# Two layers on one Trainium2 core: a group's query transfers issued earlier at the start of the attention stage, and output products and values moved in front of transposes in its last two slots

## The chip, the cores and the metric

The program runs on one core of a Trainium2 chip, in one launch, all in float32. The metric is the device time of one execution in microseconds (us). The kernel before took 937.56 us (median of three runs, 935.68 to 938.08).

The engines are named as the profile names them: PE is TensorE (PEld its weight loads), DVE is VectorE, ACT is ScalarE, POOL is GpSimd, SP is SyncE, which here only issues transfers (DMAs). Each engine works through its own list of instructions in order and waits on semaphores for the others.

## The reference, cut to what matters

The input x has 16 sequences of 256 tokens with 256 features. Two layers each compute `x = x + s * silu(f)` from the layer-normed x. In the first, s is a linear recurrence with a complex diagonal state of 32 and f is an MLP with GELU. In the second, s is attention with 16 heads whose keys and values come from a latent of 64 per token, and f is a linear layer with a routed low-rank addition. The change touches the attention only:

```
q = (x @ Wq).reshape(B, S, N_HEADS, QK_DIM)
q = concatenate([q_nope, apply_rope(q_rope)], -1)
scores = einsum('bqhd,bkhd->bhqk', q, k) * scale        # k: latent part and 64 roped features
scores = where(tril(ones((S, S))), scores, min)          # causal
attn = softmax(scores, -1)
out = einsum('bhqk,bkhd->bqhd', attn, v).reshape(B, S, N_HEADS * V_DIM)
s = out @ Wo
x = x + s * silu(f)
```

The kernel folds the key and value matrices into the query and output weights, so that queries and values live in the latent of 64.

## The kernel before, in words

The 4096 tokens are cut into 8 chunks of 512 (two sequences each). Layer 1 runs first, over all chunks. From about 276 us on the attention stage runs: for each chunk four groups of four heads, and for each group two units, one for each sequence. That is 8 units for a chunk and 64 in all, and one slot of the loop at line 1488 for each unit.

A group's queries are made on PE in four products (`query_mm`, tile pq). Two give the latent part, which ACT scales into the tile qg (`query_lat`). Two give the roped part: DVE multiplies them (`query_mul`, tile qmul), POOL adds the products into qrot (`query_rot`), and `query_move` copies qrot into the other rows of qg by eight DMAs on SP's queue. A group's queries are made in the odd slot before and the even slot of the group ahead, so group 2, which slot 4 uses first, gets its products in slots 1 and 2 and its moves in slot 2. There are two qg buffers and one for qrot.

A unit's scores come in three packs of query blocks (`score_pack`, tile sc in PSUM, three buffers): blocks 7 and 6, then 5 to 3, then 2 to 0. For each pack PE multiplies, DVE adds the mask and takes the maxima, ACT takes the exponentials into pr with their sums. DVE's reciprocal of the sums and POOL's multiplications (`normalise`) finish the probabilities.

The probabilities have to be turned before the values can be multiplied. For units 0 to 61 DVE turns 32x32 blocks (`turn`, tile turned, two buffers), SP writes them to DRAM by four DMAs (`send`, tile far), and one slot later SP reads them back by one DMA (`fetch`, tile pT, four buffers). For the last two units PE transposes them instead (`turn_here`, tile pt), and ACT and DVE copy the result to pT. `values` multiplies pT with the latent rows of the keys (tile av) and a copy writes attT. In even slots from 4 on, the values of the units four and three slots back are taken. `finish_mm` multiplies attT with the output weights (tile po, eight products of 128x256 for each 128 tokens), and `finish_out` multiplies by the gate and adds x. In the slots with r = 3, 4, 5 and 7 of a chunk this is done for one 128-token tile each of the chunk before; the last chunk's follow after the loop.

The order of the work is written by hand. The wrapper `InOrder` keeps the instructions of each engine, and SP's transfers, in the order in which the Python code calls them. All instructions of the stage therefore carry one line, L53, in the profile, and groups are told apart by their tiles. SP's order in an even slot is: the fetch of the unit two back, the four sends of the unit one back, the eight moves of the next group. In an odd slot it is a fetch and four sends.

The tiles pq, tp, pkv, pk, pm, pt, av and po share five PSUM buffers (`m1`), sc has three others, and three of the last chunk's four po tiles take sc buffers.

Of the kernel before, what the change touches and what calls it, by code (L numbers as in the profile page):

```python
# [28 lines left out]
NPAIR = NH // 2  # L29
# [12 lines left out]
def tile_two_layers(ctx: ExitStack, tc: tile.TileContext, d: dict, out: bass.AP):  # L42
# [158 lines left out]
    def bc(ap, n):  # L201

        return ap.unsqueeze(1).to_broadcast([ap.shape[0], n, ap.shape[1]])

    def bc_in(ap, n):

        return ap.unsqueeze(2).to_broadcast([ap.shape[0], ap.shape[1], n])
# [16 lines left out]
    def m1(name, shape):  # L224
        return place["pool"].tile(shape, F32, tag=place["tag"], name=name)
# [67 lines left out]
    def kv_end(ch):  # L293
        k = chunks[ch]
        sq = k.tmp[:, 0]
        ve.tensor_tensor(sq, k.pkv[:, :, 0:KVL], bc_in(k.rk, KVL), ALU.mult)
        ve.tensor_tensor(k.row[:, :, 0:KVL], sq, bc(kvw_bc, TPC), ALU.mult)
# [97 lines left out]
    def query_mul(n, t):  # L395
        q = groups[n]
        q.mul[t] = m = qm.tile([P, 2, CH], F32, tag="qmul", name=f"qmul_{n}_{t}")
        for r in range(2):
            ve.tensor_tensor(
                m[:, r, :].rearrange("p (b s) -> p b s", b=2),  # L400
                q.ps[t].rearrange("p (b s) -> p b s", b=2),
                bc(rot_q[:, r, :], 2), ALU.mult,
            )
# [15 lines left out]
    def query_move(n):  # L419
        q = groups[n]  # L420
        for r in range(2):
            for h in range(G):
                sp.dma_start(
                    q.qg[64 + 32 * r : 96 + 32 * r, :, h, :],
                    q.rot[32 * h : 32 * h + 32, r, :].rearrange("p (a q) -> p a q", q=32),
                )


    with ExitStack() as l0:
# [177 lines left out]
        for k in range(8):  # L607
            n = 1 << k
# [613 lines left out]
        ch = NCH - 1  # L1222
# [70 lines left out]
    def mid_chunk(ch):  # L1293
        k = chunks[ch]
        pmT = m1(f"pmT_{ch}", [P, CH])
        for j in range(TPC):
            pe.transpose(pmT[:, j * P : (j + 1) * P], k.mg[:, j, :], ident)
        k.mT = a2.tile([P, CH], F32, tag="mT", name=f"mT_{ch}", bufs=1)
        ac.copy(k.mT, pmT)
# [19 lines left out]
    def gate_end(ch, jp):  # L1319
        k = chunks[ch]  # L1320
        g = k.g2[:, 2 * jp : 2 * jp + 2, :]
        ve.scalar_tensor_tensor(g, g, 1.0, k.h, ALU.add, ALU.mult)
# [63 lines left out]
    def normalise(u, packs):  # L1386
        blocks = [a for pi in packs for a, _ in PACK[pi]]
        lo, hi = min(blocks), max(blocks) + 1
        ve.reciprocal(u.sr[:, lo:hi], u.sr[:, lo:hi])
        for a in blocks:  # L1390
            v = u.pr[:, OFF[a] : OFF[a] + 32 * (a + 1)]
            gp.tensor_scalar(v, v, u.sr[:, a : a + 1], 1.0, ALU.mult, ALU.mult)
# [27 lines left out]
    def new_pT(u):  # L1420
        u.pT = pp.tile([P, G, 3, P], F32, tag="pT", name=f"pT_{u.n}", bufs=4)

    def fetch(u):
        new_pT(u)
        sp.dma_start(u.pT, u.far.rearrange("k s h z q -> (k s) h z q"))

    def turn_here(u, z):

        if z == 1:
            new_pT(u)  # L1430
        a0, k0 = THIRDS[z]
        pt = m1(f"pt_{u.n}_{z}", [P, CH])
        for y in range(4):
            o = OFF[a0] + y * WID[a0] + 32 * k0
            pe.transpose(pt[:, y * P : (y + 1) * P], u.pr[:, o : o + P], ident)
        for y, e in ((0, ac.copy), (2, ve.tensor_copy)):
            e(
                u.pT[:, :, z, 32 * y : 32 * y + 64].rearrange("p h (a q) -> p a h q", q=32),
                pt[:, y * P : (y + 2) * P].rearrange("p (a h q) -> p a h q", a=2, h=G),
            )  # L1440

    def values(u, e=None):
        k, b = chunks[u.ch], u.b
        av = m1(f"av_{u.n}", [P, 2, S])
        for p2 in range(2):
            for kb in range(2):
                for hh in range(2):
                    h = 2 * p2 + hh
                    pe.matmul(
                        av[64 * hh : 64 * hh + 64, p2, P * kb : S].rearrange(  # L1450
                            "p (z s) -> p z s", s=P
                        ),
                        k.row[:, 2 * b + kb, 0:KVL],
                        u.pT[:, h, 2:3, :] if kb else u.pT[:, h, 0:2, :],
                        start=(kb == 0), stop=(kb == 1),
                    )
        if b == 0:
            k.attT.append(a2.tile([P, 2, CH], F32, tag="attT", name=f"attT_{u.n}", bufs=6))
        (e or ac.copy)(k.attT[u.g][:, :, b * S : (b + 1) * S], av)

    def finish_mm(ch, j, p0, p1):
        k = chunks[ch]
        if p0 == 0:
            if ch == NCH - 1 and j < 3:
                k.po[j] = ps_sc.tile([P, CH], F32, tag="sc", name=f"po_{ch}_{j}")
            else:
                k.po[j] = m1(f"po_{ch}_{j}", [P, CH])
        for p in range(p0, p1):
            pe.matmul(
                k.po[j][:, 0:D], k.attT[p // 2][:, p % 2, j * P : (j + 1) * P], wout[:, p, :],  # L1470
                start=(p == 0), stop=(p == NPAIR - 1),
            )

    def finish_out(ch, j, last=False):
        k = chunks[ch]
        tag, bufs = (("o", 2), ("o", 2), ("h", 1), ("tmp", 1))[j if last else 0]
        o = a2.tile([P, D], F32, tag=tag, name=f"o_{ch}_{j}", bufs=bufs)
        ve.tensor_tensor(o, k.po[j][:, 0:D], k.g2[:, j, :], ALU.mult)
        (ve if last else gp).tensor_tensor(o, o, X[ch][:, j, :], ALU.add)
        t0 = ch * CH + j * P  # L1480
        (sp if last else gp).dma_start(out_dram[t0 : t0 + P, :], o)
# [3 lines left out]
    LAST = NCH * PER  # L1485
    FINISH = (3, 4, 5, 7)
    units = [Unit(i) for i in range(LAST)]
    for i in range(LAST):
        ch, r = divmod(i, PER)
        odd = i % 2 == 1  # L1490
        u, w = units[i], units[i - 1] if i else None
        here = w is not None and w.i >= LAST - 2
        n = (i + 3) // 2 if odd else (i + 2) // 2
        n = n if n < len(groups) else None
        more = ch + 1 < NCH
        last = ch - 1 if ch and r in FINISH else None

        if 2 <= i:
            fetch(units[i - 2])
        score_pack(u, 0)  # L1500
        if w:
            normalise(w, (2,))
        if r == 1:
            gate_end(ch, 0)
        if r == 2:
            gate_end(ch, 1)
            if more and ch:
                norm_end(ch + 1)
        if r == 5 and more:
            kv_end(ch + 1)  # L1510
        if w:
            for z in (1, 2):
                turn_here(w, z) if here else turn(w, z)

        if r == 0:
            mid_chunk(ch)
        if r == 7 and more:
            key_chunk(ch + 1)
        if n is not None:
            query_mm(n, 0 if odd else 3)  # L1520
            if not odd:
                query_lat(n, 3)
        score_pack(u, 1)

        if odd and n is not None:
            query_mm(n, 1)
            query_mul(n, 0)
        if w:
            if here:
                turn_here(w, 0)  # L1530
            else:
                turn(w, 0)
                send(w)
        if not odd:
            if n is not None:
                query_move(n)
            if i >= 4:
                values(units[i - 4])
                values(units[i - 3])
        score_pack(u, 2)  # L1540
        normalise(u, (0, 1))

        if odd and n is not None:
            query_mm(n, 2)
            query_mul(n, 1)
            query_rot(n)
            query_lat(n, 2)
        if r < 2:
            gate_begin(ch, r)
        if r == 0 and more and ch:  # L1550
            norm_begin(ch + 1)
        if r == 2 and more:
            transpose_chunk(ch + 1)
        if r == 4 and more:
            kv_begin(ch + 1)
        if r == 6 and more:
            router_chunk(ch + 1)
        if last is not None:
            j = FINISH.index(r)
            finish_mm(last, j, 0, NPAIR)  # L1560
            finish_out(last, j)


    ch = NCH - 1
    u0, u1 = units[LAST - 2], units[LAST - 1]
    normalise(u1, (2,))
    turn_here(u1, 1)
    turn_here(u1, 2)
    values(units[LAST - 4])
    values(units[LAST - 3], ve.tensor_copy)  # L1570
    values(u0)
    turn_here(u1, 0)
    for j in range(TPC):
        finish_mm(ch, j, 0, 6)
    values(u1, ve.tensor_copy)
    for j in range(TPC):
        finish_mm(ch, j, 6, NPAIR)
# [76 lines left out]
```

## Time and profile before

| | |
|---|---|
| median of three runs | 937.56 us (935.68 to 938.08) |
| the profiled execution | 936.25 us, span 934.5 us |
| PE busy | 916.7 us, 98% of the span |
| DVE, POOL, ACT busy | 662.2, 471.9, 450.8 us |
| packets' time on SP's transfer queue (q1) | 52.7% of 16 engines' span |
| slot 0 to slot 8 of the attention stage | 276 to 346 us |
| slot 63 and the end | 898 to 934.5 us |

The span runs from the first to the last instruction of the profiled execution, and its time is the span and 1.75 us around it. In the timeline each row has start, length, engine, line, operation, tiles (written tile first), shape, number of records and, in brackets, the idle time of the engine before it and what ended it. A float32 matmul leaves two records on PE. A wait's releaser is inferred from the order of semaphore events; where the engine named had long been done, it was another, often a DMA. A transfer's time to landing is counted from the start of its issue.

### The profile page before, as it was taken

The page shows a single profiled execution, that of the slowest core. Times are in us where ns is not written, and L with a number is a line of the kernel's source. Part 1 is how long each engine was busy: PE and PEld are TensorE (multiplying, and loading weights), DVE is VectorE, ACT ScalarE, POOL GpSimd, SP SyncE. Part 2 cuts the span into 40 slices and gives each one's busy share as a digit, 9 for nine tenths or more (in the row PEclk, how much of TensorE's full clock was granted, in tenths as well). Part 3 has the DMA queues.
Part 4 walks back from the last instruction along what each step waited for, and adds up shares of the span by engine and source line. Part 5 has one row for each costly group of instructions (what it writes and reads, how often), then busy time and mean ns, then how long its engine had stood idle before and what let it go on. Part 6 is the DMA issues. An engine that isn't in the chain of part 4 may idle for free.

```text
span 934.5 us, 16539 instructions
## 1 busy us (share of the span) xinstructions
PE 916.7 (98%) x5066; PEld 688.2 (74%) x5066; DVE 662.2 (71%) x2005; ACT 450.8 (48%) x1495; POOL 471.9 (51%) x804
## 2 busy tenths in 40 slices
PE   8999999999999899999999999999999999999988
PEld 7765889887757567777777777777777777777766
DVE  6883668664688688678867866886886678686662
ACT  3333355554346455545645454564555456455450
POOL 1319166778255445545554554555455554645550
PEclk9999999999999999999999999999999999999999
DMA  9730000000024777776786777678677766866870
GB/s 279 224 114 1 1 1 1 1 1 1 1 32 117 182 217 199 204 178 167 174 228 164 189 195 194 165 173 230 165 197 181 197 168 169 231 166 174 224 201 29
DMA packets 196599, 133.93 MB, mean 143 GB/s; under 512 B 142304, under 2 KB 187168, under 8 KB 196512
## 3 DMA queue, kind: packets, MB, share of 16 engines
q1 hardware_dynamic: 194192, 128.68, 52.7%
q0 software_dynamic: 1344, 3.67, 1.0%
q8 instruction: 41, 0.67, 0.3%
q10 hardware_dynamic: 976, 0.53, 0.2%
q14 instruction: 46, 0.38, 0.1%
HBM read 63.11 MB, written 52.95 MB: 124 GB/s over the span
## 4 chain that ended last, share of the span: by engine, by line
PE 87%; DVE 5%; DMA 2%; SPq 2%; POOL 1%; issue 1%; ACT 1%; POOLq 0%; DVEq 0%; ACTq 0%
PE pq L53 21%; PE sc L53 14%; PE po L53 10%; PE av L53 9%; PE ph L53 6%; PE pf L53 6%; PE r L53 5%; PE pg L53 5%; PE f L53 4%; SPq L53 2%; PE pm L53 2%; PE tp L53 1%; PE pkv L53 1%; DMA far<-turned 1%; POOL pr L53 1%
## 5 line engine op out<-in xcount | busy, mean ns | idle before, releaser
L53 POOL TENSOR_SCALAR pr<-pr,sr 128x256 f32<-128x256 f32 (+7 forms) x512 | 192.5, 395 | 277.4 <-DVE sr L53 271.8
L53 ACT ACTIVATE pr<-sc,nm 128x256 f32<-128x256 f32 (+7 forms) x512 | 189.5, 380 | 279.9 <-DVE sr L53 197.0
L53 PEld LDWEIGHTS sc<-kT,qg 128*128 128x128 f32 x1024 | 159.3, 191 | 63.4 <-issue 40.0
L53 PE MATMUL sc<-kT,qg 128*128 128x256 f32 (+7 forms) x1024 | 175.7, 305 | 5.5 <-DMA qg<-qrot 2.9
L53 DVE STREAM_TRANSPOSE turned<-pr 128x512 f32<-128x512 f32 x186 | 123.3, 688 | 14.3 <-POOL pr L53 13.9
L53 DVE TENSOR_REDUCE nm<-sc 128x1 f32<-128x256 f32 (+7 forms) x512 | 127.7, 301 | 6.6
L53 PE MATMUL pq<-xnT,wlat 128*128 128x512 f32 x256 | 124.3, 609 | 0.0
L53 PE MATMUL pq<-xnT,wrope 128*128 128x512 f32 x256 | 120.2, 593 | 0.0
L53 PE MATMUL po<-wout,attT 128*128 128x256 f32 x512 | 115.8, 380 | 0.0
L53 PEld LDWEIGHTS po<-wout,attT 128*128 128x128 f32 x512 | 96.4, 190 | 20.9 <-issue 6.2
L53 ACT ACTIVATION_READ_ACCUMULATOR pr<-sc,nm 128x1 f32 x512 | 103.5, 202 | 0.0
L53 PE MATMUL av<-pT,row 128*64 128x256 f32 (+1 forms) x1024 | 90.5, 329 | 0.3 <-DMA pT<-far 0.3
L53 POOL TENSOR_TENSOR qrot<-qmul,qmul 128x512 f32<-128x512 f32 x64 | 83.4, 1324 | 5.1 <-DVE qmul L53 3.4
L53 DVE TENSOR_TENSOR sc<-sc,kmask 128x96 f32<-128x96 f32 (+1 forms) x192 | 45.9, 239 | 54.3 <-PE sc L53 52.9
L53 DVE TENSOR_TENSOR qmul<-pq,rot_q 128x512 f32<-128x512 f32 x128 | 80.9, 674 | 0.4 <-PE pq L53 0.4
L53 PEld LDWEIGHTS av<-pT,row 128*64 128x64 f32 x1024 | 64.2, 137 | 23.0 <-issue 0.5
L53 ACT ACTIVATE qg<-pq 64x512 f32<-64x512 f32 x128 | 75.4, 589 | 5.9 <-PE pq L53 5.2
L53 PEld LDWEIGHTS pq<-xnT,wlat 128*128 128x128 f32 x256 | 46.1, 192 | 32.2 <-issue 32.1
L53 PEld LDWEIGHTS pq<-xnT,wrope 128*128 128x128 f32 x256 | 45.7, 191 | 32.4 <-issue 32.1
L53 PE MATMUL ph<-xnT,p1T 128*128 128x512 f32 (+1 forms) x160 | 58.6, 524 | 0.8 <-DVE xnT L53 0.8
L53 PE MATMUL pf<-p2T,hT 128*128 128x256 f32 x256 | 56.8, 379 | 0.0
L53 PEld LDWEIGHTS pf<-p2T,hT 128*128 128x128 f32 x256 | 48.2, 190 | 7.2 <-issue 0.9
(216 smaller groups left out, 1227.2 us busy)
## 6 DMA issues: line engine op xcount, KB each, us to landing
far<-turned SPq DMA_DIRECT2D x248, 192.0 KB, 3.7
pT<-far SPq DMA_DIRECT2D x62, 768.0 KB, 4.7
qg<-qrot SPq DMA_DIRECT2D x256, 64.0 KB, 2.4
x<-in_x_dram SPq DMA_DIRECT2D x7, 512.0 KB, 9.3
out_dram<-o POOLq DMA_DIRECT2D x28, 128.0 KB, 3.3
wqn_wo<-in_wq_nopeT_dram SPq DMA_DIRECT2D x4, 512.0 KB, 4.7
wqn_wo<-in_Wo_dram SPq DMA_DIRECT2D x4, 512.0 KB, 5.8
p2T<-in_proj2T_dram SPq DMA_DIRECT2D x2, 512.0 KB, 8.0
```

Source lines behind the costliest of these rows:

```text
L53: r = getattr(self.engine, name)(*args, **kw)
```

## The change

It has three parts, all of them moves.

1. In slot 2 the eight moves of group 2 are called before the last `turn` and the `send` of unit 1. In every other even slot they stay behind the send. SP's order in slot 2 and after becomes: fetch of unit 0, eight moves, four sends of unit 1, fetch of unit 1, four sends of unit 2, and on as before.
2. In slot 63 the output products of the last 128-token tile of chunk 6, with their gate product on DVE, addition on POOL and output transfer on POOL's queue, come behind the first score pack and ahead of unit 62's transposes. Before, they came at the end of the slot.
3. After the loop, the products of four head pairs for two tiles of chunk 7 and, between them, the values of unit 60 come ahead of unit 63's transposes. The later products for these two tiles begin at the fifth pair.

```
@@ in the loop over slots, behind the first score pack
         if r == 5 and more:
             kv_end(ch + 1)
+        if i == LAST - 1:
+
+            finish_mm(last, 3, 0, NPAIR)
+            finish_out(last, 3)
+            last = None
         if w:
             for z in (1, 2):
                 turn_here(w, z) if here else turn(w, z)
@@ behind the second score pack
         if odd and n is not None:
             query_mm(n, 1)
             query_mul(n, 0)
+        if i == 2:
+            query_move(n)
         if w:
             if here:
                 turn_here(w, 0)
@@
         if not odd:
-            if n is not None:
+            if n is not None and i != 2:
                 query_move(n)
             if i >= 4:
                 values(units[i - 4])
@@ after the loop
     normalise(u1, (2,))
+
+    finish_mm(ch, 0, 0, 4)
+    values(units[LAST - 4])
+    finish_mm(ch, 1, 0, 4)
     turn_here(u1, 1)
     turn_here(u1, 2)
-    values(units[LAST - 4])
     values(units[LAST - 3], ve.tensor_copy)
     values(u0)
     turn_here(u1, 0)
     for j in range(TPC):
-        finish_mm(ch, j, 0, 6)
+        finish_mm(ch, j, 4 if j < 2 else 0, 6)
     values(u1, ve.tensor_copy)
```

More of the change, by code (lines that the diff above doesn't have):

```diff
@@ L1510, in tile_two_layers @@
             kv_end(ch + 1)
+        if i == LAST - 1:
+            finish_mm(last, 3, 0, NPAIR)
+            finish_out(last, 3)
+            last = None
         if w:
@@ L1527, in tile_two_layers @@
             query_mul(n, 0)
+        if i == 2:
+            query_move(n)
         if w:
@@ L1534, in tile_two_layers @@
         if not odd:
-            if n is not None:
+            if n is not None and i != 2:
                 query_move(n)
@@ L1566, in tile_two_layers @@
     normalise(u1, (2,))
+    finish_mm(ch, 0, 0, 4)
+    values(units[LAST - 4])
+    finish_mm(ch, 1, 0, 4)
     turn_here(u1, 1)
     turn_here(u1, 2)
-    values(units[LAST - 4])
     values(units[LAST - 3], ve.tensor_copy)
@@ L1573, in tile_two_layers @@
     for j in range(TPC):
-        finish_mm(ch, j, 0, 6)
+        finish_mm(ch, j, 4 if j < 2 else 0, 6)
     values(u1, ve.tensor_copy)
```

## The prediction, made before the changed kernel was run

> **What bounds the kernel now.** I read the page first, then TensorE's waits, then two stretches of the timeline where those waits stand.
>
> ```profile
> span 934.5 us, 16539 instructions
> PE 916.7 (98%) x5066; PEld 688.2 (74%) x5066; DVE 662.2 (71%) x2005; ACT 450.8 (48%) x1495; POOL 471.9 (51%) x804
> ...
> PE 87%; DVE 5%; DMA 2%; SPq 2%; POOL 1%; issue 1%; ACT 1%; POOLq 0%; DVEq 0%; ACTq 0%
> ```
>
> TensorE is busy 98% of the span and carries 87% of the chain that ended last. The change moves work and adds none (each engine has the same number of instructions in both programs), so it can only win or lose where TensorE waits. These are its three longest waits over the span (total, times, longest):
>
> ```profile
> PE pt L53 <- POOL pr L53: 3.2, 2, 1.9
> PE sc L53 <- DMA qg<-qrot: 2.9, 1, 2.9
> PE sc L53 <- ACT pr L53: 2.6, 3, 1.2
> ```
>
> The timeline of TensorE around them (start, length, instruction, idle before it; every matmul leaves two records, so x16 is eight matmuls):
>
> ```profile
> 304.23 1.96 PE L53 MATMUL pq<-xnT,wlat 128*128 128x512 f32 x4
> 309.11 1.10 PE L53 MATMUL sc<-kT,qg 128*128 128x256 f32 x4 [2.92 <-DMA qg<-qrot]
> 310.00 3.57 PE L53 MATMUL pq<-xnT,wlat 128*128 128x512 f32 x4
> ...
> 901.60 1.09 PE L53 MATMUL pt<-ident,pr 128*128 128x128 f32 x8 [1.85 <-POOL pr L53]
> ...
> 904.38 3.70 PE L53 MATMUL po<-wout,attT 128*128 128x256 f32 x16
> 909.38 1.09 PE L53 MATMUL pt<-ident,pr 128*128 128x128 f32 x8 [1.30 <-POOL pr L53]
> ```
>
> Slot 4 (309.11) waits 2.92 us for the third group's queries. Behind that wait four pq records take 3.57 us where the same four took 1.88 at 294.55: the granted clock is halved there. The window row (after the five busy times come clock, DMA share, GB/s):
>
> ```profile
> 310.00:312.00 2.00, 2.00 (x4) 0.96 (x3) 1.72 (x6) 0.67 (x3) 2.00 (x4) 0.50 0.90 316
> ```
>
> So this stall costs 2.92 + 1.7 = 4.6 us. The queue that feeds it is SP's:
>
> ```profile
> 295.54 0.34 SPq L53 DMA_DIRECT2D pT<-far  x1
> 299.24 2.22 SPq L53 DMA_DIRECT2D far<-turned  x4
> 301.57 5.70 SPq L53 DMA_DIRECT2D qg<-qrot  x8
> 307.32 0.62 SPq L53 DMA_DIRECT2D pT<-far  x1
> 308.03 2.40 SPq L53 DMA_DIRECT2D far<-turned  x4
> 315.95 0.34 SPq L53 DMA_DIRECT2D pT<-far  x1
> 316.39 2.81 SPq L53 DMA_DIRECT2D far<-turned  x4
> ```
>
> In slot 2 the eight moves stand behind four sends that wait for the DVE transpose ending at 299.21, though POOL finished both halves of qrot by 295.72 (293.23 + 2.49). The last move lands at 308.9, 2.3 us after its issue at 306.64.
>
> **Part one, the moves of group 2 go ahead of unit 1's sends.** What they wait for is done by 295.9: qrot at 295.72, unit 1's scores, which free the buffer, at 289.5. They issue from 295.96 and take the 5.70 of the row above (6.3 in slots 4 and 6): to 301.7. The last lands 2.3 later, about 303.4, and slot 4 can start when TensorE gets there, 306.2. Gained in slot 4: 4.6.
>
> Queued behind them on SP are the sends of unit 1. They go at 301.7 instead of 299.24. From first send to last landing four sends took 4.9 (slot 1) and 5.4 (slot 2), so the fetch of unit 1 goes at 306.6 to 307.1, against 307.32 before. It is hardly moved, since it no longer stands behind the eight moves. It lands 4.2 after issue when alone (slot 2) and 5.0 to 5.7 with sends close behind (slots 4 and 6): 311.6 to 312.8. TensorE reaches unit 1's values in slot 4 at about 310.9 (306.1, plus 2.5 from first to second score pack as in slot 2, 0.9 to the values, 1.4 for unit 0's), so a new wait of 0.7 to 1.9 stands there; I take 1.2.
>
> Then SP's own chain sets slot 6. From that fetch to the landing of unit 2's sends took 7.7 in slot 4 without moves in front (315.95 to 323.69) and 8.5 in slot 3 with them (307.32 to 315.81). Without them now: from 307.0 to 314.5, and the next fetch follows at 314.6 instead of 315.95. Unit 3's sends and group 3's eight moves hang on it at fixed distances, so group 3 lands at 325.9, not 327.24, and slot 6 starts 1.3 earlier than its 327.65. TensorE would be there 4.6 - 1.2 = 3.4 earlier. So about two thirds of what slot 4 wins comes back as a wait of 2 to 3 us in slot 6. By slot 8, which also waited for its moves (1.22, put down to ACT, but the last move landed at 345.4 and the pack began at 345.81), the same sums give 1.5 earlier; if the clock falls behind the new wait, 0.6. I take 1.4 for the whole part. From slot 10 to slot 60 TensorE waits for no moves and simply starts earlier. Bounds: 6.2 if every one of these waits goes (4.6, slot 6's 0.41, slot 8's 1.22), and -2.8 by the longest rows: moves 6.3, sends landing 7.8 after the first (slot 3), 8.5 from fetch to the next landing, so 302.3 + 7.8 + 8.5 = 318.6 against 315.81.
>
> [...]
>
> **Part two, slot 63 takes the output products of chunk 6 first.** They are 16 records, 3.5 to 3.7 us, and now stand where TensorE sat idle for 1.85. What is queued behind them (transposes of unit 62, scores and normalisation of unit 63) starts 1.6 to 1.85 later. DVE's product (0.42) and POOL's add and output transfer (0.73 + 0.30 + 0.59) move with them; POOL is idle from 902.8 to 907.6, so they lie beside.
>
> **Part three, the tail.** From unit 62's transposes to unit 63's, 901.60 to 909.38, runs a chain over DVE, ACT and POOL of 7.78 us; TensorE has 2.78 of its own in it and 5.0 to be filled. Before, the products filled it but for 1.30. Now eight records each for two chunk-7 tiles (48 took 10.53, so 1.75 each) and unit 60's values (48 took 4.12, so 1.37) fill 4.9. About 0.1 to 0.2 of wait is left. They need attT of groups 0 and 1, units 60's pT (fetched two slots before) and three score buffers, all free by then. The rest of the tail holds the same matmuls less these, so the end comes 3.15 - 0.15 = 3.0 earlier. Bounds: 3.15, and 0.8 if POOL's 1.62 and ACT's copy of unit 60's values (0.58), which now stand ahead of unit 63's pieces, lengthened the chain.
>
> **Sum.** The profiled execution took 936.25 (span 934.50 and 1.75 around it). 936.25 - 1.4 - 3.0 = 931.85. The median of the three runs is 937.56, 1.31 above it, so I forecast 933.2.
>
> **Rivals.**
> - The queries' stall goes for good: the fetches land early enough that slots 6 and 8 do not wait. 6.2 + 3.0 gives 928.4. For it: DMA has room (its share was 0.10 in 314 to 316). Against: SP's fetch in an even slot waits for sends issued just before it, and that latency stays.
> - The stall only moves to slot 6, nothing is left of part one: 937.56 - 3.0 = 934.6. For it: DMA share 0.90 to 1.03 from 308 to 314, so the transfers may be limited by their amount, and the amount is unchanged. [...] Against: the engines idled from 314 to 317 while SP waited.
> - The tail's cover fails: POOL's add and transfer or ACT's copy hold up unit 63, 2.2 of the 3.0 comes back: 935.4. Against: POOL had 4.88 us idle before that normalisation.
> - Slower: unit 1's probabilities come late. If its sends land x later than 306.9, slot 4's values wait and all of SP's chain to slot 8 comes x later, one for one. From x = 4.4 the gain of both parts is gone, from 7.2 it is 0.3% slower; x = 7.5 gives 940.7. The longest row (7.8 from first send to last landing, against 4.9) gives x = 2.9 only.
>
> **How the numbers follow.** About 0.3%, 2.8 us, is what a measurement of this kernel can tell from no change: 934.75 below. Forecast 0.55 (own range 931 to 934.7); stall gone 0.10; stall moved 0.15; tail fails 0.12; slower 0.08. Faster: 0.55 + 0.10 + half of 0.15 = 0.72; within 0.3%: the other half and 0.12, 0.20; slower 0.08. The range leaves out the first rival and the slower one (0.18): 930.0 to 936.5, which also holds the runs' own spread of 1.2 each way.
>
> **What would show it.** In the profile after: the eight moves directly behind the fetch at 295.5; no wait for qg at slot 4, full clock from 306 to 314; a short wait for pT in slot 4's values; a wait of 2 to 3 us for qg at slot 6, shorter at slot 8; then everything 1 to 2 us earlier. At the end, no TensorE wait before unit 62's transposes and at most 0.3 before unit 63's. I am wrong if slot 6's wait takes all that slot 4 gave, or if unit 63's transposes still wait over 1 us.

## The result, and the profile after

The changed kernel took 934.23 us (median of nine runs, 932.55 to 936.55). The kernel before, run beside it, took 936.88 us (nine runs, 935.68 to 938.08). The ratio is 0.9973 with a 95% interval of 0.9962 to 0.9983, so about 2.6 us were won. The forecast had 933.2 and a gain of 4.4. The profiled execution took 934.0 us.

The head of the page of the changed kernel, and the shares of its chain:

```profile
span 932.2 us, 16540 instructions
PE 915.6 (98%) x5066; PEld 688.3 (74%) x5066; DVE 662.4 (71%) x2005; ACT 451.6 (48%) x1495; POOL 473.2 (51%) x804
...
PE 91%; DVE 4%; DMA 2%; SPq 1%; ACT 0%; POOL 0%; issue 0%; DVEq 0%; POOLq 0%; ACTq 0%
```

TensorE's longest waits in it (total, times, longest):

```profile
PE sc L53 <- ACT pr L53: 3.8, 2, 2.0
PE av L53 <- DMA pT<-far: 3.5, 1, 3.5
PE tp L53 <- DVE xn L53: 2.0, 1, 2.0
```

The two waits before transposes (pt) and the one for the queries (qg) are gone from the top of the list. In their place stand one for unit 1's probabilities (pT) and two before score packs (the third row, tp, is a wait at 7 us, when the program starts). The timeline of TensorE shows where:

```profile
305.62 0.97 PE L53 MATMUL sc<-kT,qg 128*128 128x256 f32 x4
306.43 1.88 PE L53 MATMUL pq<-xnT,wlat 128*128 128x512 f32 x4
...
314.06 1.52 PE L53 MATMUL av<-pT,row 128*64 128x256 f32 x16 [3.47 <-DMA pT<-far]
...
327.54 1.05 PE L53 MATMUL sc<-kT,qg 128*128 128x256 f32 x4 [1.86 <-ACT pr L53]
...
346.44 1.70 PE L53 MATMUL sc<-kT,qg 128*128 128x256 f32 x4 [1.96 <-ACT pr L53]
...
904.04 1.04 PE L53 MATMUL pt<-ident,pr 128*128 128x128 f32 x8
...
906.76 1.97 PE L53 MATMUL po<-wout,attT 128*128 128x256 f32 x8
908.66 1.52 PE L53 MATMUL av<-pT,row 128*64 128x256 f32 x16
910.11 1.99 PE L53 MATMUL po<-wout,attT 128*128 128x256 f32 x8
911.94 1.04 PE L53 MATMUL pt<-ident,pr 128*128 128x128 f32 x8
```

Slot 4 starts at 305.62 without a wait and its four pq records take 1.88 us, at the full clock. But its second block of values (314.06) waits 3.47, slot 6 (327.54) waits 1.86 and slot 8 (346.44) waits 1.96. The profile puts these two down to ACT, but the last moves of their groups landed at 327.13 and 345.99, just before the packs began. At the end neither the transposes of unit 62 (904.04) nor those of unit 63 (911.94) wait. Behind slot 8's wait the clock is halved, as the window row shows (after the five busy times: clock, DMA share, GB/s):

```profile
348.00:350.00 2.00, 2.00 (x7) 1.47 (x6) 1.97 (x6) 1.91 (x8) 2.00 (x5) 0.50 0.93 297
```

SP's own timeline, from the fetch of unit 0 on:

```profile
295.09 0.34 SPq L53 DMA_DIRECT2D pT<-far  x1
295.59 6.34 SPq L53 DMA_DIRECT2D qg<-qrot  x8
302.04 2.47 SPq L53 DMA_DIRECT2D far<-turned  x4
309.01 0.34 SPq L53 DMA_DIRECT2D pT<-far  x1
309.45 2.39 SPq L53 DMA_DIRECT2D far<-turned  x4
315.97 0.34 SPq L53 DMA_DIRECT2D pT<-far  x1
316.35 2.55 SPq L53 DMA_DIRECT2D far<-turned  x4
319.02 6.48 SPq L53 DMA_DIRECT2D qg<-qrot  x8
```

The eight moves now stand behind the fetch at 295.09, and the four sends of unit 1 behind them. The fetch of unit 1 goes 13.92 us after the fetch of unit 0; before, it was 11.78 (307.32 - 295.54).

**Where the time went.** A slot's start is taken as that of its first score pack (sc, 128x256). The table gives, stretch by stretch and in us, how much longer (+) or shorter (-) each profiled execution was than that of the kernel before; the rows add up to the difference of the spans. The first column is what layer 1 and the start leave, which no edit but one touches: it spreads over 1.7 us by itself.

| kernel | to slot 0 | slot 0 to 12 | slot 12 to 63 | slot 63 to end | span |
|---|---|---|---|---|---|
| changed kernel | -0.41 | +2.72 | -1.31 | -3.25 | -2.25 |
| changed kernel, again | -0.85 | +2.55 | -0.42 | -3.22 | -1.94 |
| part one alone | +0.72 | +0.17 | +0.02 | 0.00 | +0.91 |
| parts two and three | +0.36 | +0.10 | +0.76 | -3.24 | -2.02 |
| part two alone | -1.01 | -0.02 | +0.42 | +4.17 | +3.56 |
| part three alone | +0.29 | -0.01 | +0.28 | -1.18 | -0.62 |
| moves, values later | -0.79 | -1.13 | -0.06 | +1.45 | -0.53 |
| moves first | +0.55 | +0.33 | +0.13 | -3.23 | -2.22 |
| moves first, values later | +0.38 | -0.09 | +0.34 | -3.25 | -2.63 |
| four warm-up products | -0.02 | -0.50 | -1.05 | -3.23 | -4.80 |
| unit 1 left out | -0.71 | -4.70 | +0.31 | -3.38 | -8.48 |
| two queues, slot 2 new | +0.21 | -3.17 | -1.16 | -2.85 | -6.97 |
| two queues, slot 2 old | -0.79 | -1.59 | -1.32 | -2.84 | -6.54 |

The last slot wins 2.8 to 3.4 wherever parts two and three stand together, 3.2 in most. The first slots of the attention stage, where part one should have won, lost 2.7 and 2.6 in the two profiled executions of the changed kernel, and won 0.5 in the one with four warm-up products, whose order is the same. The third stretch holds two small waits, ahead of slot 62 and inside it (0.93 and 0.27 before), that are there in some executions and not in others, without a cause that I could name.

### The profile page after: what moved, and what is told of

It reads as the page before. It is cut to its first block, busy times and chain, and to the rows that moved or that the text cites. A ratio compares the mean times of both kernels' runs of the same rounds, so it can differ in the third digit from the quotient of the medians.

```text
span 932.2 us, 16540 instructions
## 1 busy us (share of the span) xinstructions
PE 915.6 (98%) x5066; PEld 688.3 (74%) x5066; DVE 662.4 (71%) x2005; ACT 451.6 (48%) x1495; POOL 473.2 (51%) x804
## 3 DMA queue, kind: packets, MB, share of 16 engines
q0 software_dynamic: 1344, 3.67, 1.1%
## 4 chain that ended last, share of the span: by engine, by line
PE 91%; DVE 4%; DMA 2%; SPq 1%; ACT 0%; POOL 0%; issue 0%; DVEq 0%; POOLq 0%; ACTq 0%
PE pq L53 21%; PE sc L53 15%; PE po L53 12%; PE av L53 9%; PE ph L53 6%; PE pf L53 6%; PE r L53 5%; PE f L53 4%; PE pg L53 4%; PE pm L53 1%; PE pkv L53 1%; PE tp L53 1%; SPq L53 1%; DMA far<-turned 1%; PE pb L53 1%; PE psq L53 1%
```

## Experiments

Each was run on the chip beside the kernel before; ratios are to it, with 95% intervals.

**The parts by themselves.** Part one alone leaves out the two other hunks of the diff.

```
+        if i == 2:
+            query_move(n)
...
-            if n is not None:
+            if n is not None and i != 2:
                 query_move(n)
```

> Only group 2's moves go ahead of unit 1's sends; the end is as before. Theory A (the prediction): slot 4's stall of 4.6 us goes, most of it comes back at slots 6 and 8, and 1.4 us is left: 935.5 us against 936.9. Theory B (from the profile after the whole change): the wait for unit 1's probabilities (3.5 us in slot 4) and longer waits at slots 6 and 8 (1.9 and 2.0 us) with one stretch of half clock take more than the stall was worth: slot 9 starts 2.3 us later than before; the waits before slots 62 and 63 (0.93 and 0.27 us) take up 1.2 of it, so 938.0 us, 1.1 slower.

Measured: 937.35 against 936.81, ratio 1.0002 (0.9988 to 1.0016). Part one is worth nothing that can be told from noise: the interval reaches from 1.1 us won to 1.5 lost, and the 1.4 of the forecast lies just outside it. Its timeline of TensorE in slots 4 and 5:

```profile
307.56 1.88 PE L53 MATMUL pq<-xnT,wlat 128*128 128x512 f32 x4
...
313.81 2.17 PE L53 MATMUL av<-pT,row 128*64 128x256 f32 x16 [2.11 <-DVE turned L53]
...
317.21 3.76 PE L53 MATMUL pkv<-wkva,xnT 128*128 128x128 f32 x16
```

The wait for the queries is gone, the one for unit 1's probabilities is 2.11 (put down to DVE; the fetch landed at 313.68, just before it ended). It is shorter than the 2.92 that it replaces, yet the halved clock behind it lasts twice as long: 6.83 us from 314.54, where before it was 3.41. The pkv records take 3.76 instead of the 2.03 of the changed kernel. Slot 4 starts 3.08 earlier than before, counted from slot 0, and slot 5 starts 0.42 later.

Parts two and three, without part one:

```
+        if i == LAST - 1:
+            finish_mm(last, 3, 0, NPAIR)
+            finish_out(last, 3)
+            last = None
...
+    finish_mm(ch, 0, 0, 4)
+    values(units[LAST - 4])
+    finish_mm(ch, 1, 0, 4)
...
```

> Only the reordering of slot 63 and behind the loop; slot 2 is as before. Theory A: 3.0 us less, as the whole change gave 2.7 and the moves give 1.4 that would then be missing: between 932.5 and 934. Theory B: the two waits of 1.85 and 1.30 us go and nothing is lost at the start: 3.2 to 3.5 us less, 933.5 us, so this part alone is faster than both parts together by 0.5 to 1 us.

Measured: 933.96, ratio 0.9971 (0.9956 to 0.9985). As far as the intervals tell, that is all of the whole change's gain (0.9973). The stall of slot 4 is still there (2.9 for qg), and no transposes wait at the end.

Part two alone has the first of these hunks, part three alone the second.

> Only chunk 6's last output products are moved ahead of unit 62's transposes; behind the loop all is as before. Both theories: the wait of 1.85 us before unit 62's transposes goes, but the products no longer fill the time before unit 63's transposes, where 5.0 us of chain had 3.5 us of products and 1.3 us of wait: that wait grows to 4.8 us. Net 0 to 0.3 us slower or no change: 936.6 to 937.2 us. If it were faster by over 1 us, the parts would be independent and the fill would come from elsewhere.

Measured: 940.28, ratio 1.003 (1.0017 to 1.0043), 3.5 us slower by the medians, where no change or 0.3 had been expected. Its timeline of TensorE at the end:

```profile
902.43 1.04 PE L53 MATMUL pt<-ident,pr 128*128 128x128 f32 x8
...
910.16 1.97 PE L53 MATMUL pt<-ident,pr 128*128 128x128 f32 x8 [4.85 <-POOL pr L53]
912.06 6.00 PE L53 MATMUL av<-pT,row 128*64 128x256 f32 x48
```

and its window behind the wait:

```profile
910.00:915.00 5.00, 4.84 (x26) 3.67 (x28) 0.85 (x2) 0.81 (x3) 1.33 (x5) 0.50 0.00 0
```

The products filled the 1.85 before unit 62's transposes, and the same products were then missing before unit 63's, which wait 4.85 instead of 1.30: waiting grew by 1.7 in all. The rest of the 4.17 of this execution is the clock, halved from 909.09 for 6.83 us; 48 av records take 6.00 where the forecast had read 4.12.

> Only the products of four pairs for two tiles and unit 60's values go ahead of unit 63's transposes; slot 63 is as before. Both theories: the wait of 1.30 us before unit 63's transposes goes (8.3 us of work now stands where 5.0 are needed), the wait of 1.85 us in slot 63 stays: 1.3 us less, 935.6 us. With the last-slot part it should add up to the end alone only if the two parts need each other: 1.3 plus about 0 is less than 3.2.

Measured: 935.5, a median 1.3 lower, as expected; the interval of the ratio, 0.9976 (0.9962 to 0.999), reaches from 0.9 to 3.6 us won. Unit 62's transposes still wait 1.86, unit 63's no more. Part three is worth its own 1.3 with part two absent, and 6.3 us where part two has opened the hole (940.28 to 933.96). The two parts are one edit: part two takes the cover from the second gap, part three lays another one there.

**Is it the wait of slot 4's values?** If part one fails because slot 4 must wait for unit 1's probabilities, taking these values later should set it free. Part one with the values of units 0 and 1 in slot 5:

```
-            if i >= 4:
+            if i >= 4 and i not in LATER:      # LATER = (4,)
                 values(units[i - 4])
...
+        if odd and i - 1 in LATER:
+            values(units[i - 5])
+            values(units[i - 4])
```

> Group 2's moves ahead of unit 1's sends, without the parts at the end, and the values of units 0 and 1 taken in slot 5 and not in slot 4, so that nothing in slot 4 waits for late probabilities. If unit 1's late probabilities are what costs the gain of the moves (2.1 to 3.5 us of wait in slot 4 and the half clock behind it), this gains 2 to 4.6 us on the kernel before: 932 to 935 us. If SP's chain of fetches that wait for sends sets the pace, group 3's moves land at about the same time (326.9 to 327.2) and the wait only moves to slot 6, 4 to 5 us long: no change against before, 936 to 938 us.

Measured: 935.84, ratio 0.999 (0.9977 to 1.0003). The waiting row of TensorE's timeline in slots 4 to 8 is now a single one:

```profile
325.17 1.05 PE L53 MATMUL sc<-kT,qg 128*128 128x256 f32 x4 [3.57 <-DMA qg<-qrot]
```

TensorE runs through slot 4 and waits in slot 6 instead, for group 3's queries, with a halved clock behind (326.47, 3.41 us). By slot 12 1.13 are won. In this execution the last slot gave 1.45 back: there the clock was halved behind the old 1.86 us wait before unit 62's transposes, which before did not bring it.

Next, the whole change with group 3's, 4's and 5's moves ahead of the fetch in slots 4, 6 and 8 as well, without and with the values put later. If SP's order decides, this frees slots 6 and 8; if the amount of transfers does, it can't.

```
+        if i in EARLY:                         # EARLY = (4, 6, 8)
+            query_move(n)
...
-            if n is not None and i != 2:
+            if n is not None and i != 2 and i not in EARLY:
```

> The whole change, and in slots 4, 6 and 8 the eight moves also stand first on SP, ahead of the fetch that waits for the landing of the sends just before it. Same transfers, same bytes. If the chain of fetches behind sends sets the pace, group 3's moves are issued at about 310 to 312 us instead of 319, land 6 to 8 us earlier, and slots 6 and 8 wait for no moves; the wait for unit 1's probabilities in slot 4 (2.1 to 3.5 us) stays: 2 to 4 us less than the whole change, 930 to 932 us. If the amount of transfers sets the pace, the fetches and sends come later by what the moves come earlier, TensorE waits for probabilities instead, and it stays at 934 us.

> As the kernel with the moves first, and the values of units 0 and 1 taken in slot 5. If the chain of fetches is the cause, neither queries nor probabilities are waited for between slots 4 and 8: all of 6.2 us at the start and 2.8 at the end are won, 928 to 929 us. If the amount of transfers sets the pace, a wait of 3 us or more stands somewhere from slot 5 to slot 8, and it is 932 us or more.

Measured: 933.67, ratio 0.9961 (0.9946 to 0.9975), and 933.49, ratio 0.997 (0.9958 to 0.9982). Neither is apart from the whole change. The first has no wait before slots 6 and 8; it waits for probabilities instead, 3.32 in slot 4 and 1.79 in slot 8. The second waits 2.94 for probabilities in slot 6, and its halved clock lasts 6.83 us. So three orders more only gave other places for a wait. The last two came out as had been expected for a limit by the amount of transfers; the runs with two queues below speak against that limit.

**What is it that takes the time?** One link of SP's sequence left out altogether: the whole change without unit 1's sends and fetch, with unit 0's probabilities used in unit 1's values.

```
-        if 2 <= i:
+        if i == 3:
+            units[1].pT = units[0].pT
+        elif 2 <= i:
             fetch(units[i - 2])
...
-                send(w)
+                if w.i != 1:
+                    send(w)
```

> The whole change, with unit 1's four sends and its fetch left out (0.77 MB each way); its values are multiplied with unit 0's probabilities instead, so that part of the output is not the reference's. All products remain. If SP's chain of fetches behind sends sets the pace from slot 2 to slot 8, one link of about 7 us is gone: unit 2's sends go at 305.5 (when they are turned) instead of 309.4, no wait in slot 4, group 3's moves land 3 us earlier or more and slot 6 waits less than 1 us; 2 to 5 us less than the whole change, 929.5 to 932 us. If something on TensorE, DVE or POOL sets the pace of the first slots, the waits stay at other places and it is 934 us.

Measured: 928.32, ratio 0.9922 (0.9908 to 0.9936), some 0.5% below the whole change. Slot 4 does not wait, slots 6 and 8 wait 1.02 and 0.76, and the clock stays full from slot 0 to slot 63:

```profile
322.70 1.05 PE L53 MATMUL sc<-kT,qg 128*128 128x256 f32 x4 [1.02 <-DMA qg<-qrot]
340.41 1.05 PE L53 MATMUL sc<-kT,qg 128*128 128x256 f32 x4 [0.76 <-DMA qg<-qrot]
```

So the transfers of these slots set the pace. By amount or by their sequence? With half of the moves of groups 2, 3 and 4 on ACT's queue the amount is the same, and SP's sequence is shorter:

```
-                sp.dma_start(
+                (ac if r and 2 <= n <= 4 else sp).dma_start(
```

> The whole change, with four of the eight moves of groups 2, 3 and 4 issued on ACT's queue instead of SP's. Bytes and packets are the same; SP issues 2.5 us less in every second slot. If SP's time to issue is part of the limit, the two-slot cycle of 17.1 to 18.5 us between fetches falls by about 2 us and 1 to 4 us are won against the whole change, 930 to 933 us. If the landing of sends and fetches alone sets the pace, the cycle stays and ACT's exponentials come 2.5 us later besides: 934 to 936 us.

Measured, on the whole change: 931.9 against 936.12, ratio 0.9952 (0.9938 to 0.9967), an interval that still touches the changed kernel's (0.9962 to 0.9983). TensorE's waits in slots 4 to 8 of its profiled execution:

```profile
313.00 1.52 PE L53 MATMUL av<-pT,row 128*64 128x256 f32 x16 [1.80 <-DMA pT<-far]
325.55 1.05 PE L53 MATMUL sc<-kT,qg 128*128 128x256 f32 x4 [0.94 <-DVE sc L53]
342.85 1.05 PE L53 MATMUL sc<-kT,qg 128*128 128x256 f32 x4 [0.36 <-DVE nm L53]
```

The same with slot 2 in the old order, that is parts two and three with two queues, and beside it the changed kernel again:

> The parts at the end, and four of the eight moves of groups 2, 3 and 4 on ACT's queue, with slot 2 in the order of the kernel before (unit 1's sends ahead of SP's four moves). If the order in slot 2 is worth nothing and the split does the work, this is as fast as the split with the moves ahead (931.9 us, 0.9952 of before) or faster by up to 2 us, since unit 1's fetch goes 3 us earlier and slot 4's values wait for nothing, while the last of the moves lands at about 306: 930 to 932 us. If the moves must go first for slot 4, slot 4 waits 1 to 3 us for queries and it is 932.5 us or more.

> The changed kernel again, on the same chip as the kernel with two queues, for a direct comparison: 0.9973 of before (0.9962 to 0.9983) as at first, 933.5 to 934.5 us.

Measured against 937.01: 929.76, ratio 0.992 (0.9905 to 0.9936), for the first, and 934.36, ratio 0.9963 (0.9949 to 0.9978), for the changed kernel. The version with two queues and the old order beats both kernels, by 7.2 and 4.6 us. TensorE's waits in slots 3 to 8 of it:

```profile
303.72 0.86 PE L53 MATMUL sc<-kT,qg 128*128 128x96 f32 x6 [0.70 <-ACT pr L53]
307.99 1.05 PE L53 MATMUL sc<-kT,qg 128*128 128x256 f32 x4 [1.62 <-DMA qg<-qrot]
325.34 1.05 PE L53 MATMUL sc<-kT,qg 128*128 128x256 f32 x4 [0.91 <-DVE qmul L53]
343.43 1.05 PE L53 MATMUL sc<-kT,qg 128*128 128x256 f32 x4 [1.15 <-DMA qg<-qrot]
```

and SP's timeline:

```profile
294.73 0.34 SPq L53 DMA_DIRECT2D pT<-far  x1
298.45 4.02 SPq L53 DMA_DIRECT2D far<-turned  x4
303.55 2.61 SPq L53 DMA_DIRECT2D qg<-qrot  x4
306.32 0.50 SPq L53 DMA_DIRECT2D pT<-far  x1
```

SP issues four moves in 2.61 us where it had eight in 5.70 (the four sends ahead of them, issued while ACT issues its four, take 4.02 instead of 2.22), and the wait of slot 4 falls from 2.92 to 1.62. No halved clock follows, which before cost 1.7. The windows from 308 to 344 us of this kernel, and then of the kernel before, carry nearly the same transfers per us:

```profile
308.00:344.00 36.00, 33.94 (x199) 23.62 (x200) 29.04 (x101) 20.52 (x81) 18.49 (x38) 1.00 0.78 207
```

```profile
308.00:344.00 36.00, 34.49 (x196) 23.68 (x196) 25.21 (x88) 18.25 (x69) 17.43 (x36) 0.95 0.77 204
```

(DMA share 0.78 and 0.77, 207 and 204 GB/s.) Over a fifth of the transfer engines' time is free in both on the average, so the amount of bytes alone does not bound these slots; in single windows of 2 us the share does reach 1.01 and 1.03 (308 to 310 and 312 to 314 before). The intervals of the two versions with two queues just miss each other (0.9936 and 0.9938), on different chips. Which order of slot 2 is the better one there stays open: the medians speak for the old order, but in the profiled executions the new one won 3.17 from slot 0 to slot 12 and the old one 1.59. The profiled execution of the new order was the fastest of its six (929.57, the others up to 934.21).

**One late landing.** In the profile after, the fourth send of unit 1 landed 2.55 us after the third, where a step is 0.7 to 1.3 in the profile before, and a 16 KB read of instructions ran on the transfer engines at 306.93. To shift that read against the sends, the program was made shorter ahead of them: four warm-up products instead of eight.

```
-NWARM = 8
+NWARM = 4
```

> The whole change with 4 instead of 8 warm-up products at the very start, so that TensorE's later instructions stand 16 places earlier in its list. In the profile after, one 16 KB instruction read on the transfer engines at 306.9 us coincided with the last of unit 1's sends, which landed 2.55 us after the third instead of 0.75. If the read delays the landing, it now falls about 1.5 us later against the slots, after the sends have landed: the fourth lands about 0.8 us after the third, the fetch goes about 2 us earlier and slot 4's wait is 1.5 to 2 us instead of 3.5. If the coincidence is by chance, slot 4 waits 3 us or more as before. The time itself says little, since the start is changed.

Measured in a single run: 931.45. The read came at 306.36 and the fourth send still 1.64 after the third. But with the values put later (the second group of experiments) such a read at 306.49 overlapped that landing and it came 0.69 after the third.

The 14 profiled executions together say more. Take the step from one send's landing to the next of the same unit. Of the 2230 steps beside which no instruction read ran, or one of 8 KB alone, the median is 0.69 us and the longest 1.49. Of the 344 steps beside which 16 KB or more were read, 114 took 1.5 us or more, up to 2.59. So every long step stood beside such a read, and 230 of the 344 steps beside 16 KB or more stayed under 1.5 us. What it is that holds up the send, the runs do not show. With group 2's moves ahead on one queue, unit 1's fourth send came 1.64 to 2.55 after the third in four executions (the changed kernel twice, moves first, four warm-up products), and unit 1's fetch then went 13.12 to 13.92 after unit 0's. In the three others (part one alone, and the two with values later) it was 0.69 to 0.97, and 12.12 to 12.20.

## Why the prediction was right or wrong

The time lay in the range and the direction was right; the gain was forecast as 4.4 and measured as 2.6, because part one, one of the forecast's two terms, came out at nothing. That the time still lay in the range says nothing for part one: the range, 930.0 to 936.5, also held the 934.6 of the rival in which part one is worth nothing. The forecast named as a sign of being wrong that slot 6's wait takes all that slot 4 gave, and so it came.

**Parts two and three: right.** The forecast had 3.0 between 0.8 and 3.15. The medians give 2.85 (936.81 to 933.96), and the last slot of the profiled executions gives 3.2, a little over the upper bound. No wait is left before either transposes; I had kept 0.1 to 0.2. The rival "the tail's cover fails" (0.12) falls: POOL's addition and output transfer run at 904.75 and 905.77, and POOL then still waits 3.67 us for unit 63's normalisation.

**Part one, step by step.**
- The moves go from 295.59 in the changed kernel and their issue ends at 301.93; forecast 295.96 and 301.7. The last landed at 303.74; forecast 303.4. Slot 4's wait is gone and the clock is full. All right.
- "The fetch of unit 1 goes at 306.6 to 307.1", that is 11.1 to 11.6 after unit 0's fetch. Measured: 13.92 in the changed kernel, 13.47 when it was run again, 12.20 with part one alone. This term was mis-sized. Between the two fetches stand the moves, 6.9 to the first send instead of 6.2, and the sends, 6.95 to the last landing in the changed kernel instead of 4.9 to 5.4 (5.29 with part one alone). The first excess is there every time; the second goes with the late landing of the fourth send, beside an instruction read.
- The wait for unit 1's values was taken as 1.2. It is 3.47, 3.18 and 2.11 in the same three executions.
- From the fetch of unit 1 to that of unit 2 I took 7.6; it is 6.96 (7.26 with part one alone). From there group 3 was to keep its distance of 11.29 and took 11.16. These links were right, but they hang on the late fetch, and group 3 landed 0.1 earlier than before (327.13 against 327.24), not 1.3.
- The wait in slot 6 was forecast as 2 to 3 and is 1.86. Slot 5 had still started 1.16 earlier than before, counted from slot 0; slot 6 starts 0.30 later, so all that slot 4 had won is gone. Slot 8 was to start 1.5 earlier (0.6 with a halved clock); it starts 1.04 later and then runs at half the clock. From the fetch of unit 3 to that of unit 4 SP took 9.09 instead of 7.78, a link which I had held fixed; among unit 4's sends there one landed 2.03 after the one before, again beside an instruction read.
- "I take 1.4 for the whole part" is the step that failed. Part one alone measured 1.0002, and it was the rival "the stall only moves", to which I had given 0.15 and 934.6 us, that came true. Its reason, the amount of transfers, is not borne out: with two queues the same bytes went through sooner.
- The rival "Slower: unit 1's probabilities come late" had the mechanism, and took each microsecond after 306.9 that the sends land as one lost. On the time of the kernel before (counted from slot 0) they landed at 309.40 in the changed kernel, 2.5 late, and at 307.73 with part one alone, 0.8 late. By its rule 1.9 is left of the 4.4; 2.6 was measured.

**What stands in its place.** The transfers of slots 2 to 8 set these slots: without unit 1's sends and fetch 4.70 us are won there. On SP each fetch waits for the landing of its unit's sends (111.2 us of waiting in all in the kernel before, up to 5.4 at once), the sends wait for DVE's turns (30.1 in all, up to 7.0), and sends and moves stand behind the fetch before. The table takes the stretch from slot 0 to slot 12 apart (profiled executions, us). Idle time and clock together give the differences to the kernel before to within 0.41.

| kernel | slot 0 to 12 | TensorE idle in it | lost to the halved clock | fetch of unit 0 to fetch of unit 5 |
|---|---|---|---|---|
| before | 108.65 | 5.02 | 1.71 | 48.16 |
| parts two and three | +0.10 | 5.12 | 1.71 | 48.30 |
| part one alone | +0.17 | 3.90 | 3.41 | 48.34 |
| changed kernel | +2.72 | 7.77 | 1.71 | 49.25 |
| changed kernel, again | +2.55 | 7.59 | 1.71 | 49.01 |
| moves, values later | -1.13 | 4.14 | 1.71 | 46.42 |
| moves first | +0.33 | 5.59 | 1.71 | 50.61 |
| moves first, values later | -0.09 | 3.57 | 3.41 | 47.63 |
| two queues, slot 2 new | -3.17 | 3.57 | 0 | 45.45 |
| two queues, slot 2 old | -1.59 | 4.85 | 0 | 47.03 |
| unit 1 left out | -4.70 | 2.26 | 0 | |

Part one alone did take 1.12 us of idle time out of these slots, not far from the 1.4 of the forecast, but 1.70 more of halved clock took it back. SP's sequence has no fixed length: other orders on one queue gave 46.42 to 50.61, and none of them gained anything that can be told from noise. With two queues and the old order TensorE waits hardly less than before (4.85 against 5.02), only in smaller pieces, so that its 1.59 are the clock; with the new order both idle time and clock fall. What part of SP's time is issue, what the order of landing within a queue, and what full transfer engines, the runs do not separate.

Why only these slots? They are the short ones. In the changed kernel slots 2 and 3 hold 12.29 us of TensorE's work, slots 4 and 5 16.59 and slots 6 and 7 16.94 without their waits, and from fetch to fetch SP took 17.47 to 18.32 for two slots before. From slot 8 to slot 58 two slots take 18.69 us or more. Slots 60 and 61 take 16.17 again, so the small waits at slot 62 fit the same cause; this was not tested.

**The clock, a cost that I had tied to the wrong thing.** I counted 1.7 for the clock that slot 4 had lost and nothing for its new wait. With part one alone a wait of 2.11 brought 6.83 us at half speed, of which 6.23 lay before slot 5 (314.54 to 320.77) and cost half of that, 3.1. The sum for slot 5 is then -3.08 + 2.11 - 1.7 + 3.1 = 0.43 later, and 0.42 was measured.

## What to carry to other kernels

When TensorE waits for a transfer on a queue whose entries wait for each other, add up the queue from end to end before changing its order: if the sum stays, the wait only moves. Here fewer entries helped, and so did a second queue, though for that one the traces show only part of the reason. Work moved into one idle gap is taken from the place that it covered, so the two gaps are costed together: here the first move alone lost 3.5 us and the pair won 2.9. A wait can have a second price, the halved clock behind it, and that is read wait by wait: here the changed kernel paid 3.41 us at half speed behind its wait of 1.96 us and nothing behind that of 3.47.

## What the runs showed of the hardware

**Where the halved clock fell.** In the changed kernel's execution the stretches of halved clock begin at 8.77, 346.69 and 930.37 us, 99 and 171 times 3.413 us apart, and the first two last 3.413 each. In that of the kernel before one begins at 309.97 and lasts 3.413, and the next record of a halved clock stands at 934.61, 183 such steps later. If the time of each of these two executions between 20 and 915 us is cut at these steps, the three pieces with most idle time of TensorE hold 2.55 us (of the 2.92 before slot 4 in the kernel before), 1.97 (part of the 3.47 us wait of the changed kernel, whose other 1.50 lay in the next piece) and 1.96 (before slot 8 in the changed kernel). The clock was halved right behind the first and the third, and not behind the second. So in these two executions the length of a wait alone did not tell whether a halved clock came.

In the profiled executions of other runs one came behind waits of 2.11 us (6.83 us long, part one alone), 3.57 (3.41, moves with the values later) and 4.85 (6.83, part two alone), and none behind the longest waits that the two versions with two queues have in slots 3 to 8, 1.80 and 1.62 (the clock is 1.00 there from 308 to 326). Of two waits of 1.86 us before unit 62's transposes one was followed by it (moves with the values later) and one was not (part three alone, where 24 po records behind it took 5.43 us, as 16 take 3.62 in the changed kernel).

**A second issuing queue.** The time that SP takes to issue was not small here: in the kernel before and in the changed kernel the eight moves took it 5.70 to 6.74 us, and in slot 2 of the kernel before the last one landed 2.3 us after its issue. With half of them on ACT the ratio is 0.992, and 0.9971 without (parts two and three). Not all of that is traced to the queue: of the 4.5 us between these two profiled executions 1.7 lie between slots 0 and 12, as much as the halved clock cost there; 1.2 lie ahead of slot 0 and 2.1 behind slot 12, where the edit changes nothing.
